# Loading the rows of the projection's first half in two parts

## The chip, the cores and the metric

The kernel runs on one core of a Trainium2 chip. A core has a matrix engine (TensorE, PE in the profile, its weight loads PEld), three engines for element-wise work (VectorE, DVE; ScalarE, ACT; GpSimd, POOL), a sync engine (SyncE, SP) that here only issues transfers, and 16 DMA engines that move data between HBM (DRAM) and the on-chip memory SBUF. Matmul results go to PSUM banks. Each engine takes its own instructions in order and waits for others by semaphores. The metric is the device time of one execution in microseconds.

## The reference

The input `x` is 32 images of 96 channels by 56 by 56, in float32. Two layers run on it, one after the other.

```
layer 0:  h = silu(bn1(conv1x1(x, w1)))            # 96 -> 576 channels
          h = silu(bn2(depthwise3x3(h, w2)))
          s = sigmoid(se2 @ silu(se1 @ mean(h)))    # squeeze and excite, per image
          x1 = x + bn3(conv1x1(h * s, w3))          # 576 -> 96: "the projection"
layer 1:  ca, sa = channel and spatial gates from |rfft2(x1)|, mean and norm of x1
          y  = x1 * ca * sa
          offset, gate, y_base = 3x3 convolutions of y (and of coordinates and |rfft2(y)|)
          y_def = deformable 3x3 convolution of y at the offsets
          z  = (1 - gate) * y_base + gate * y_def
          out = relu(batchnorm over all images (z) + x1)
```

## The kernel before

An image goes through three stages, and the stages of successive images run beside each other. `hidden` (L204) expands and convolves the 576 hidden channels of image b+2. `attend` (L447) projects image b+1 back to 96 channels and works out its gates with Fourier sums. The main loop in `layers` (L953) does the offsets, the sampling and the deformable convolution of image b, in 7 bands of 8 rows. The main loop is cut into slots: after each small piece of the image's own work, `pump` advances the other two stages by a step, so that every engine holds a mixture of the three in an order that is fixed when the program is built. SP's transfers stand in the order in which they are written, too.

**Hidden stage.** The 576 channels are held in nine units (`UNITS`, L75): channels 0 to 511 of the upper half of the image (units 0 to 3), a mixed unit of the last 64 channels with both halves (unit 4), and channels 0 to 511 of the lower half (units 5 to 8). Each unit ends in `acch`, 128 partitions by 28 rows by 56, which ACT finishes (L222) and stores to the DRAM tile `h2d` (L224).

**Projection.** It takes four steps, q = 0 to 3, of seven rows of the upper and seven of the lower half. `project_loads` (L307) brings the rows back: with `half` 0 it loads units 0 to 3 into `hq0` (128 x 4 x 392, 784 KB) and with `half` 1 units 4 to 8 into `hq1` (128 x 5 x 392, 980 KB). Both tiles have one buffer, so the load for q+1 waits until TensorE has read that of q. `project` (L321) multiplies: at L329 four matmuls over `hq0` into one PSUM bank, a step later four over units 5 to 8 of `hq1` into a second bank, then the two of unit 4 (L335). The profile has two records for each such matmul, so that a group of four shows as x8. ACT adds the bias (L339), POOL adds `x` (L476).

In `attend` the order is: matmuls of `hq0`, then the load of the next `hq0`, then the matmuls of `hq1`, then the load of the next `hq1`.

**Sampling weights.** For each band, `offsets` (L654) stores the offsets to DRAM (L668) and loads them back spread over 112 partitions as `ht` (L680, 252 KB). ACT makes hat functions `ho` of it (L686, L688) and stores them as `hd` (L690). `weights_load` (L696) loads them back as `wc` (two loads, L702) and `wr` (L703); VectorE multiplies the two (L709). The sources of `ht` and `wc` are broadcast over a leading dimension of eight. Matmuls at L738 sample with the product, ACT copies the samples into `v` (L742, L749), and L757 is the deformable convolution into the PSUM tile `pd`, of which there is one. VectorE reads `pd` into `z` (L796 to L799), and only then can the matmuls of the next band at L757 write `pd`.

**Transfers.** SP issues the loads of `hq0`, `hq1`, `xt`, `yp`, `ht`, `wc`, `wr` on one queue (q1), ACT the stores of `h2d` and `hd` on another (q10), POOL the rest (q0). SP and ACT share eight completion semaphores in rotation: a transfer waits until the one that stands eight places before it has landed.

Of the kernel before, what the change touches and what calls it, by code (L numbers as in the profile page):

```python
# [33 lines left out]
EW = ER * W  # L34
# [267 lines left out]
def project_rows(p, half):  # L302

    return p["hq"].tile([128, (NCH - 1, len(UNITS) - NCH + 1)[half], EW], FP, name=f"hq{half}")


def project_loads(nc, p, h2d, q, half):  # L307

    u0, u1 = ((0, NCH - 1), (NCH - 1, len(UNITS)))[half]
    hq = project_rows(p, half)  # L310
    nc.sync.dma_start(hq, h2d[u0:u1, :, q * EW : (q + 1) * EW].rearrange("u p n -> p u n"))
    return [(UNITS[u][0], hq[:, u - u0]) for u in range(u0, u1)]


# [132 lines left out]
def attend(tc, p, b, x, h2d, pooled, x1, given=False):  # L447
# [7 lines left out]
    if not given:  # L455
        NQ = HH // ER
        first = project_loads(nc, p, h2d, 0, 0)
        yield from squeeze(nc, p, pooled)
        rows = [first, project_loads(nc, p, h2d, 0, 1)]
        for _ in range(2):  # L460
            yield
        for q in range(NQ):
            at = q, q + NQ
            xrs = [residual_load(nc, p, x, k) for k in at]
            outs = project(nc, p, rows)
            next(outs)
            yield
            if q + 1 < NQ:
                first = project_loads(nc, p, h2d, q + 1, 0)
            yield  # L470
            os = next(outs)
            if q + 1 < NQ:
                rows = [first, project_loads(nc, p, h2d, q + 1, 1)]
            yield
            for k, o, xr in zip(at, os, xrs):
                nc.gpsimd.tensor_tensor(o, o, xr, ALU.add)  # L476
                nc.gpsimd.dma_start(x1[:, k * EW : (k + 1) * EW], o)
            yield
# [1037 lines left out]
```

## Time and profile before

| | |
|---|---|
| three runs | 8979.61, 9001.68, 9002.55 us; median 9001.68 us |
| profiled execution | 8993.57 us, span on the core 8991.8 us |
| mean granted TensorE clock | 0.94 |
| PE busy | 8180.0 us (91% of the span) |
| VectorE busy | 7174.8 us (80%) |
| ScalarE busy | 5380.8 us (60%) |
| GpSimd busy | 2600.4 us (29%) |
| loads of hq0, hq1 | 128 of 784 KB, 128 of 980 KB |
| matmuls at L329 | 2048 records, 796.8 us busy, 99.2 us of idle time before them |

An image takes some 262 us (q = 3 of images 15 and 16 starts at 4157.98 and 4417.24 us). A line of the table of groups or of the timeline gives start, duration, engine, source line, operation and tiles out<-in; a number in square brackets is the idle time of that engine just before, and what is taken to have ended it. A line of the waits gives who waited for whom, microseconds in total, how often, and the longest. Releasers are inferred from semaphore events: a wait for several is put down to the last event that is seen, and that is not always the right one. "Granted clock" is the share of full speed that TensorE is given. Images are counted from 0.

### The profile page before, as it was taken

How to read it: one execution, taken by the hardware profiler on the slowest of the kernel's cores; microseconds unless marked ns; L12 is line 12 of the kernel's file. 1: busy time of each engine (PE TensorE's matmuls, PEld its weight loads, DVE VectorE, ACT ScalarE, POOL GpSimd, SP SyncE). 2: the span in 40 equal slices, each digit the busy share in tenths (PEclk: the TensorE clock that was granted, in tenths of full speed). 3: DMA queues.
4: the chain of work that ended last, by engine and by line, in shares of the span. 5: the costliest groups of instructions: out<-in, count | busy, mean ns of one | idle time of the engine just before them, and what ended most of it. 6: DMA issues, size and time to landing. Idle time of an engine off the chain costs nothing. (4 is left out here: it accounts for less than half of the span.)

```text
span 8991.8 us, 137403 instructions
## 1 busy us (share of the span) xinstructions
PE 8180.0 (91%) x52406; PEld 5185.1 (58%) x52406; DVE 7174.8 (80%) x6821; ACT 5380.8 (60%) x10486; POOL 2600.4 (29%) x2608
## 2 busy tenths in 40 slices
PE   5899999999999999999999999999999999999960
PEld 3456565666656656665666666566566656666640
DVE  7688888888888888888888888888888888887333
ACT  2356666666666666666666666666666666666553
POOL 0133233333323332332332333233333323332210
PEclk9889999999999999999999999999999999999985
DMA  2356666666666666666666666666666666666669
GB/s 80 109 144 167 164 167 164 164 155 155 169 167 167 169 163 150 159 164 167 169 167 160 153 159 166 168 167 168 164 151 162 166 166 168 168 165 146 130 189 417
DMA packets 1068756, 1486.47 MB, mean 165 GB/s; under 512 B 590190, under 2 KB 839838, under 8 KB 1055806
## 3 DMA queue, kind: packets, MB, share of 16 engines
q1 hardware_dynamic: 858995, 985.20, 46.7%
q10 hardware_dynamic: 153803, 329.80, 10.2%
q0 software_dynamic: 55296, 162.60, 6.7%
q8 instruction: 420, 6.88, 0.4%
q14 instruction: 242, 1.98, 0.1%
HBM read 1064.29 MB, written 412.65 MB: 164 GB/s over the span
## 5 line engine op out<-in xcount | busy, mean ns | idle before, releaser
L262 DVE SCALAR_TENSOR_TENSOR acch<-hp,w,acch 128x1512 f32<-128x1512 f32 (+1 forms) x2250 | 4348.3, 1933 | 38.3
L615 PE MATMUL mm<-yp,c_jointW 104*128 104x448 f32 x4032 | 1655.9, 562 | 1.0 <-DMA yp<-fqd 1.0
L720 POOL COPY ybl<-yp 96x448 f32<-96x448 f32 x896 | 1035.1, 1183 | 1541.2 <-PE mm L724 1541.0
L757 PE MATMUL pd<-v,c_def 128*96 128x224 f32 (+1 forms) x6272 | 1429.6, 375 | 53.8 <-DVE z L796 29.0
L757 PEld LDWEIGHTS pd<-v,c_def 128*96 128x96 f32 (+1 forms) x6272 | 1039.5, 173 | 349.1 <-issue 74.5
L615 PEld LDWEIGHTS mm<-yp,c_jointW 104*128 104x128 f32 x4032 | 768.0, 194 | 758.2 <-issue 724.7
L738 PE MATMUL mm<-wc,yt 64*96 64x144 f32 x12544 | 1086.6, 302 | 115.7 <-ACT yb L649 44.8
L738 PEld LDWEIGHTS mm<-wc,yt 64*96 64x96 f32 x12544 | 845.6, 165 | 430.2 <-issue 193.2
L173 ACT ACTIVATE hp<-mm,sh,inv 128x392 f32<-128x392 f32 (+2 forms) x1216 | 812.0, 672 | 461.9 <-PE mm L169 416.4
L169 PE MATMUL mm<-xt,w 96*128 96x392 f32 (+3 forms) x2688 | 1056.8, 527 | 34.4 <-DMA xt<-in_x 33.4
L742 ACT COPY v<-mm 96x288 f32<-96x288 f32 (+1 forms) x2688 | 1003.6, 442 | 126.9 <-PE mm L738 81.4
L329 PE MATMUL mm<-hq,w3s 128*96 128x392 f32 x2048 | 796.8, 536 | 99.2 <-DMA hq<-h2d 92.4
L709 DVE TENSOR_TENSOR wc<-wc,wr 128x1008 f32<-128x1008 f32 x448 | 562.7, 1256 | 365.8 <-DMA wr<-hd 338.6
L644 PE MATMUL mm<-yp,c_base0W 96*64 96x224 f32 x8064 | 827.3, 357 | 0.0
L668 POOL DMA_DIRECT2D od<-at x224 | 185.6, 829 | 2217.9 <-DVE at L664 1515.6
L749 ACT COPY v<-v 32x448 f32<-32x448 f32 x1344 | 755.2, 562 | 29.7
L644 PEld LDWEIGHTS mm<-yp,c_base0W 96*64 96x64 f32 x8064 | 554.0, 135 | 275.4 <-issue 61.5
L726 ACT COPY yt<-mm 128x384 f32<-128x384 f32 (+1 forms) x896 | 350.5, 439 | 544.3 <-PE mm L724 543.8
L635 ACT ACTIVATE hid<-mm,c_dg1b 50x448 f32<-50x448 f32 x224 | 140.6, 628 | 862.9 <-PE mm L615 853.6
L329 PEld LDWEIGHTS mm<-hq,w3s 128*96 128x96 f32 x2048 | 339.1, 174 | 453.1 <-issue 311.0
L222 ACT ACTIVATE acch<-acch,sh,inv 128x1568 f32<-128x1568 f32 x288 | 488.3, 1695 | 180.3 <-DVE acch L262 167.0
L476 POOL TENSOR_TENSOR o<-o,xc 96x392 f32<-96x392 f32 x256 | 374.3, 1462 | 738.9 <-ACT o L339 737.3
(194 smaller groups left out, 9146.8 us busy)
## 6 DMA issues: line engine op xcount, KB each, us to landing
h2d<-acch ACTq DMA_DIRECT2D x288, 784.0 KB
wc<-hd SPq DMA_DIRECT2D x896, 252.0 KB
wr<-hd SPq DMA_DIRECT2D x448, 504.0 KB
hq<-h2d SPq DMA_DIRECT2D x128, 980.0 KB
hq<-h2d SPq DMA_DIRECT2D x128, 784.0 KB
hq<-x1d SPq DMA_DIRECT2D x768, 98.0 KB
ht<-od SPq DMA_DIRECT2D x224, 252.0 KB
hd<-ho ACTq DMA_DIRECT2D x224, 252.0 KB
```

The source lines that it names most:

```text
L169: nc.tensor.matmul(pt[p0 : p0 + w1.shape[1], : rows * W], w1, xts[hf][:, r0 * W : (r0 + rows) * W], start=True, stop=True)
L173: nc.scalar.activation(h1[lo:hi, row0 : row0 + rows, 1 : 1 + W], pt[lo:hi, : rows * W].rearrange("p (h w) -> p h w", h=rows), AF.Silu, bia ...
L262: nc.vector.scalar_tensor_tensor(acc[:, lo:hi], win, wk, acc[:, lo:hi], ALU.mult, ALU.add)
L329: nc.tensor.matmul(pts[half][:C, :EW], w3s[:, ch], hq, start=(i == 0), stop=False)
L615: nc.tensor.matmul(view, weights[:, k], yp[:channels, r0 : r0 + RB, dx + PD - 1 : dx + PD - 1 + W], start=(k == 0), stop=(k == NTAP - 1))
L644: nc.tensor.matmul(pb[i * BC : (i + 1) * BC, : BW // 2].rearrange("p (h w) -> p h w", h=RB // 2), w["base"][:, k], yp[:C, r0 + i * RB // 2 ...
L709: p["tc"].keep_in_program_order(nc.vector.tensor_tensor(wc, wc, wr, ALU.mult))
L720: nc.gpsimd.tensor_copy(yb[:, :, s], blocks)
L738: nc.tensor.matmul(pt[k][:C, (t - lo) * KP : (t - lo + 1) * KP], yt[ps, t], s[ps, t * KP : (t + 1) * KP], start=True, stop=True)
L742: nc.scalar.copy(v[:C, :, lo:hi, k].rearrange("c k t p -> c t k p"), pt[k][:C, : (hi - lo) * KP].rearrange("c (t k p) -> c t k p", t=hi - ...
L749: nc.scalar.copy(v[C:, 1 + 2 * i : 3 + 2 * i], v[i * QC : (i + 1) * QC, KA:])
L757: nc.tensor.matmul(out.rearrange("c q (t x) -> c t q x", x=TS), p["w"]["def"][ks, k], v[ks, k].rearrange("c t s (r x) -> c t (s r) x", r=T ...
```

## The change

The load of `hq0` is issued as two transfers, of units 0 and 1 and of units 2 and 3, one after the other on the same queue. The load of `hq1` remains one.

```
     u0, u1 = ((0, NCH - 1), (NCH - 1, len(UNITS)))[half]
     hq = project_rows(p, half)
-    nc.sync.dma_start(hq, h2d[u0:u1, :, q * EW : (q + 1) * EW].rearrange("u p n -> p u n"))
+    for u, v in ((u0, u1),) if half else ((u0, u0 + 2), (u0 + 2, u1)):
+        nc.sync.dma_start(hq[:, u - u0 : v - u0], h2d[u:v, :, q * EW : (q + 1) * EW].rearrange("u p n -> p u n"))
     return [(UNITS[u][0], hq[:, u - u0]) for u in range(u0, u1)]
```

In the built program the order of the instructions on PE, DVE, ACT and POOL is the same as before. SP has 128 more transfers. The first matmul of each L329 group over `hq0` waits for the first part alone; the third one, the first to read unit 2, has a wait for the second part.

## Prediction

> **What bounds the kernel now.** I read the shares and the clock of the page first, then the waits, then one image in the timeline (image 16, around q = 3).
>
> ```profile
> PE 8180.0 (91%) x52406; PEld 5185.1 (58%) x52406; DVE 7174.8 (80%) x6821; ACT 5380.8 (60%) x10486; POOL 2600.4 (29%) x2608
> ...
> PEclk9889999999999999999999999999999999999985
> ...
> L329 PE MATMUL mm<-hq,w3s 128*96 128x392 f32 x2048 | 796.8, 536 | 99.2 <-DMA hq<-h2d 92.4
> ```
>
> TensorE is nearly always busy at nearly full clock, so time saved on it counts, if nothing else is late next. Its longest wait for a transfer is the one that the change touches: 92.4 us in 30 waits of about 3.1 us.
>
> The timeline of PE, SP, ACT and DVE in image 16 shows where that wait stands, and what runs beside it:
>
> ```profile
> 4386.43 12.84 SPq L311 DMA_DIRECT2D hq<-h2d  x2
> 4401.30 0.66 SPq L680 DMA_DIRECT2D ht<-od  x1
> 4404.94 9.08 SPq L311 DMA_DIRECT2D hq<-h2d  x2
> 4428.75 1.20 SPq L702 DMA_DIRECT2D wc<-hd  x2
> 4430.04 0.54 SPq L703 DMA_DIRECT2D wr<-hd  x1
> ...
> 4409.89 2.87 PE L329 MATMUL mm<-hq,w3s 128*96 128x392 f32 x8
> 4417.24 4.36 PE L329 MATMUL mm<-hq,w3s 128*96 128x392 f32 x8 [2.79 <-DMA hq<-h2d]
> 4447.51 0.94 PE L757 MATMUL pd<-v,c_def 96*96 96x224 f32 x2 [2.30 <-ACT v L749]
> ...
> 4415.30 0.78 ACT L686 ACTIVATE ho<-ht,c_blk 112x576 f32<-112x576 f32 x1 [2.77 <-DMA ht<-od]
> ...
> 4439.56 1.21 DVE L709 TENSOR_TENSOR wc<-wc,wr 128x1008 f32<-128x1008 f32 x1 [3.35 <-DMA wr<-hd]
> 4440.69 5.97 DVE L262 SCALAR_TENSOR_TENSOR acch<-hp,w,acch 128x1568 f32<-128x1568 f32 x3
> 4446.69 0.68 DVE L796 SCALAR_TENSOR_TENSOR z<-pd,c_cvec,yb 96x448 f32<-96x448 f32 x1
> ```
>
> Two things are to be seen. First, the load for q = 3, issued at 4404.94, is 12.3 us under way and TensorE waits for it; a group of eight records that takes 2.87 us elsewhere takes 4.36 us after the pause. Second, 30 us later TensorE waits again, at L757, until VectorE has read `pd` into `z` (the group names ACT, but z ends at 4447.37 and L757 starts at 4447.51). VectorE was late because it waited at 4439.56 for `wr`, and `wr` hangs on a chain of transfers: `ht` issued 4401.30, `ho` at 4415.30, `hd` stored, `wc` and `wr` issued from 4428.75. Nothing in that chain asks for the matmuls of q = 3.
>
> The granted clock around the two pauses (columns: window, its length, busy time of PE, PEld, DVE, ACT, POOL, clock, DMA share, GB/s):
>
> ```profile
> 4416.90:4420.31 3.41, 3.07 (x5) 1.53 (x6) 3.37 (x2) 1.70 (x3) 2.49 (x3) 0.50 1.16 279
> 4420.31:4447.62 27.31, 25.01 (x140) 14.51 (x139) 21.85 (x21) 11.88 (x23) 12.79 (x14) 1.00 0.74 176
> 4447.62:4454.45 6.83, 6.83 (x23) 5.23 (x24) 6.16 (x9) 2.71 (x6) 1.57 (x3) 0.50 1.06 226
> ```
>
> Each pause is paid twice, once as idle time and once as a clock of 0.5 for 3.41 or 6.83 us.
>
> **The change part by part.**
>
> *Issues on SP.* 128 more issues of 0.37 us (median of the 256 at L311) are 47 us of SP's time. Cover: after `hq0` SP stands at the load of `hq1`, which waits for L335 (758.1 us in 96 waits) or for the last `h2d` store. If that cover went, `hq1` would be issued 0.4 us later, and over images 2 to 30 it lands at least 2.6 us before it is read (q = 2; 9 us and more at the others). Cost 0. Bytes and packets are unchanged, and q1 takes them in order.
>
> *Rotation of the semaphores.* With a transfer more, the `wr` issued at 4416.68 would wait for the first part of `hq0` in place of `ht`; the whole `hq0` had landed by 4417.1, so it is at most 0.5 us late, and VectorE multiplies it only at 4432.53. Cost 0.
>
> *The added wait on the third matmul.* Matmuls with a wait already satisfied follow the one before in 329 ns at L246, as those without one do. Cost 0 where the second part has landed.
>
> *q = 0 to 2.* The last packet of `hq0` has passed 16.3 us (q = 0), 8.7 us (q = 1) and 9.5 us (q = 2) before TensorE reads it, in medians over images 2 to 30. No gain.
>
> *q = 3, the earlier start.* TensorE is ready 9.5 us after the issue in each of these images; the wait is 2.43 to 4.11 us, mean 3.15. How much earlier does half the load land? Of the 16 completion marks of this load, one for each DMA engine, eight come about 8 us after the issue and eight only at 11.2 to 12.2 us (image 16). The late eight are held by `ht`, whose packets run until about 9.5 us; their 256 packets of `hq0` pass between about 9.0 and 11.1 us, half of them by about 10.2 us (sums over images 2 to 30). So the first part should land 0.9 us sooner. Bounds: 0 (both parts end with one late engine) and 3.15 us (it lands before TensorE is ready). I take 0.9, since the late engines' packets are the nearest row. The first two matmuls then take 1.3 us (4 of 8 records of 2.87 us, in their spacing of 0.33) or 2.6 us at half clock, longer than 0.9, so the second part is there when the third matmul comes. A shorter pause also has less slow clock: pauses of 2.4 to 2.5 us had 3.41 us of it, the mean over all is 5.06. At 0.44 us lost for each us (image 16: 4.36 - 2.87 = 1.49 us in 3.41) I put this at 0.4. Gain on TensorE 1.3 us an image.
>
> *What is late next.* `z` starts 7.1 us after the product at L709 at the earliest (1.21 and 5.97 us of VectorE). Over images 2 to 30 that limit is met exactly in about half, and `z` comes later than it by 7.9 us in all. So the earlier TensorE can advance L757 by 8 us at most over the run; the rest of 29 x 1.3 = 38 us is waited for at L757. Gain 8 us.
>
> *The clock after L757.* The pause there is 1.31 us now in the mean (0.56 to 3.05) and becomes 1.31 + 1.3 - 0.27 = 2.3 us. Of the nine pauses there of 1.41 to 1.49 us, five brought the slow clock, and all of 2.3 us and over did. Slow time after L757 is now 2.24 us an image; pauses of 2.4 to 2.8 us at q = 3 had 4.7, so for 2.3 I take 4.3. Cost 29 x 0.44 x (4.3 - 2.24) = 26 us. Bounds: 0, and 58 us if each image gets 6.83 us.
>
> *What absorbs it.* 140 us later TensorE waits for VectorE at L724 (19.1 us in 13 waits, 1.5 us each). There a delay of 0.9 us disappears in 13 images: 12 us. Bounds 0 and 26.
>
> Sum: -8 + 26 - 12 = +6 us. On the profiled execution's 8993.57 us this is about 9000 us; the median of the runs is 8.1 us above it, so 9008 us.
>
> **Two rules of the Trainium skill.** The trace has slow clock after pauses of 1.41 to 2.0 us, and its stretches are multiples of 3.41 us. The skill's page "TensorE: Matmul & The Clock Gate" (section on HAM oscillation) gives the same 3.4 us window, but as a rule for authors to have "no PE-idle gaps >~3.4µs". By that rule a pause of 2.3 us would cost no clock, and the sum would be -8 us; the trace decides against it. The page "DMA: Bandwidth & Descriptors" (Rules for kernel authors, and Anatomy of one DMA) speaks against the change: it advises to join transfers, up to 1 MiB each, and counts about 2 us as fixed for each. Estimated from that page, a second part landing 2 us after the whole load does now would be about 0.3 us late at half clock, +9 us in 30 waits; no row here shows such a cost.
>
> **The rivals.**
>
> *The gain reaches the end (faster).* If `z` is not what holds L757, or the chain of `ht`, `hd` and `wr` moves up as well, 1.3 us x 30 = 39 us are saved: 8963 us. For it speaks TensorE's 91%; against it the wait at L757 in nearly every image. A first part landing before TensorE is ready would free 3.15 + 2.0 us, 154 us in all; the late engines exclude most of that.
>
> *The clock after L757 (slower).* Place: L757, 30 us after q = 3. Price: up to 58 us with 6.83 us of slow clock in each image and nothing absorbed, less 8: 9052 us. It decides from 5.0 us of slow time an image: 29 x 0.44 x (5.0 - 2.24) = 35, less 8, is 27 us. For it: every pause of 2.3 us and more has at least one slow window. Against it: the later waits for VectorE.
>
> *Nothing happens.* Both parts land together because the last completion mark comes from one late engine: 0 us, 9002 us.
>
> **How the numbers follow.** A measurement can tell about 0.3%, 27 us, from no change. Chances: my sum 0.28 and "nothing" 0.15, both within it; the slower rival 0.32; the faster 0.25. The 80% range leaves about a tenth out beyond each rival: 8960 to 9046 us; my sum's own range is 8990 to 9027.
>
> **What the changed profile would show.** The wait of L329 for `hq` falls from 3.1 to about 2.2 us, in 30 waits still at q = 3; the third matmul has no wait of its own; the wait at L757 grows by about 1 us and shows slow clock in more than the present 12 images; `wr` lands at the same distance from the load of q = 3. The prediction is wrong if L329's wait vanishes, if the third matmul waits, or if L757 keeps its pause while the image gets shorter.

## The result, and the profile after

The changed kernel takes 9030.81 us (median of six runs, 9021.72 to 9035.16) beside 8994.65 us for the kernel before on the same chip: a ratio of 1.0044, 95% interval 1.0031 to 1.0058, or 36 us more. A second measurement, taken with the experiments below, gave 1.0039 (1.0024 to 1.0054). The change makes the kernel slower by 0.4%.

From L312 on, the changed kernel's lines stand one lower than those of before: L330 is the old L329, L758 the old L757, L797 the old L796. From the page, the shares of the engines and the two groups that changed:

```profile
PE 8191.1 (91%) x52406; PEld 5199.6 (58%) x52406; DVE 7176.8 (80%) x6821; ACT 5384.4 (60%) x10486; POOL 2612.2 (29%) x2608
...
L758 PE MATMUL pd<-v,c_def 128*96 128x224 f32 (+1 forms) x6272 | 1458.7, 380 | 112.2 <-DVE z L797 93.2
...
L330 PE MATMUL mm<-hq,w3s 128*96 128x392 f32 x2048 | 763.2, 517 | 65.1 <-DMA hq<-h2d 33.5
```

The line of the deformable convolution in the page of before:

```profile
L757 PE MATMUL pd<-v,c_def 128*96 128x224 f32 (+1 forms) x6272 | 1429.6, 375 | 53.8 <-DVE z L796 29.0
```

Before, L329 had 796.8 us of work with 99.2 us of idle time ahead of it; now it is 763.2 and 65.1. The projection has become 68 us cheaper. L757 had 1429.6 and 53.8 us; L758 has 1458.7 and 112.2, which is 87 us dearer. That is the case in two lines: the deformable convolution has lost more than the projection has gained.

The waits of TensorE (who for whom: us in all, times, longest) say who does it:

```profile
PE pd L758 <- DVE z L797: 93.2, 30, 5.6
...
PE mm L330 <- DMA hq<-h2d: 33.5, 14, 5.2
PE mm L330 <- ACT ho L687: 30.2, 17, 3.0
```

Two waits of before, for this section and a later one:

```profile
PE pd L757 <- DVE z L796: 29.0, 25, 3.0
...
PE mm L738 <- DVE sq L379: 17.6, 13, 4.9
```

So the wait for `z` was 29.0 us. Of the three lines of after, the second and the third are one wait: both stand at q = 3 and are for the first part of `hq0`. In every image from 2 to 29 the group starts 0.14 us after a completion mark of that part, as it did before after one of the whole load; where an operation of `ho` ends between the two, the profile names `ho`.

Image 16 in the timeline, PE first and then VectorE:

```profile
4439.62 4.54 PE L330 MATMUL mm<-hq,w3s 128*96 128x392 f32 x8 [1.89 <-ACT ho L687]
4452.51 2.88 PE L330 MATMUL mm<-hq,w3s 128*96 128x392 f32 x8
4470.31 0.59 PE L758 MATMUL pd<-v,c_def 96*96 96x224 f32 x2 [2.54 <-DVE z L797]
...
4462.35 1.21 DVE L710 TENSOR_TENSOR wc<-wc,wr 128x1008 f32<-128x1008 f32 x1 [2.64 <-DMA wr<-hd]
4463.48 5.97 DVE L262 SCALAR_TENSOR_TENSOR acch<-hp,w,acch 128x1568 f32<-128x1568 f32 x3
4469.48 0.68 DVE L797 SCALAR_TENSOR_TENSOR z<-pd,c_cvec,yb 96x448 f32<-96x448 f32 x1
```

TensorE now waits 1.89 us at q = 3. The third matmul of the group has no wait of its own: the whole group stands in one line with one idle time. Thirty us later the chain is the old one: VectorE waits for `wr`, then does the product and three long operations, and only then `z`. TensorE is held until `pd` has been read into `z`, in this image for 2.54 us. The clock around the two pauses (window, its length, busy time of PE, PEld, DVE, ACT, POOL, clock, DMA share, GB/s):

```profile
4440.12:4443.53 3.41, 3.41 (x7) 1.46 (x6) 3.38 (x2) 1.96 (x4) 2.25 (x3) 0.50 1.14 299
4443.53:4470.84 27.31, 24.77 (x141) 14.53 (x140) 24.31 (x22) 12.55 (x24) 13.58 (x14) 1.00 0.68 171
4470.84:4477.67 6.83, 6.83 (x24) 4.91 (x22) 5.69 (x9) 1.92 (x5) 1.57 (x3) 0.50 0.98 223
```

I followed TensorE through each image by the number of its instruction and took means over images 2 to 29. Positions count from the moment when TensorE is ready for q = 3, and "lead" is how much earlier than before it reaches the same instruction (minus is earlier):

| | before | after | after, repeat |
|---|---|---|---|
| pause at q = 3, us | 3.18 | 1.98 | 2.20 |
| slow clock within the next 40 records, us | 5.12 | 1.95 | 2.56 |
| lead 40 records after q = 3, us | 0 | -2.45 | -1.96 |
| pause at the deformable convolution, us | 1.30 | 3.34 | 3.03 |
| slow clock from it to record 200, us | 2.19 | 5.97 | 5.12 |
| lead at record 200, us | 0 | +0.90 | +0.84 |
| length of an image against before, us | 0 | +1.17 | +0.94 |

The pause and its slow clock were not removed. They moved 30 us down the image. The lead is used up at `z`, which does not come earlier, and the longer pause there brings more slow clock than it did. Some 29 images of 1.17 us are 34 us; the profiled executions differ by 33 us (spans 9025.0 and 8991.8).

### The profile page after: what moved, and what is told of

The parts are those of the page before. It is cut to its first block, busy times and chain, and to the rows that moved or that the text cites. A ratio compares the mean times of both kernels' runs of the same rounds, so it can differ in the third digit from the quotient of the medians.

```text
span 9025.0 us, 137505 instructions
## 1 busy us (share of the span) xinstructions
PE 8191.1 (91%) x52406; PEld 5199.6 (58%) x52406; DVE 7176.8 (80%) x6821; ACT 5384.4 (60%) x10486; POOL 2612.2 (29%) x2608
## 2 busy tenths in 40 slices
DMA packets 1070806, 1486.49 MB, mean 165 GB/s; under 512 B 592238, under 2 KB 841886, under 8 KB 1057854
## 5 line engine op out<-in xcount | busy, mean ns | idle before, releaser
L758 PE MATMUL pd<-v,c_def 128*96 128x224 f32 (+1 forms) x6272 | 1458.7, 380 | 112.2 <-DVE z L797 93.2
L758 PEld LDWEIGHTS pd<-v,c_def 128*96 128x96 f32 (+1 forms) x6272 | 1056.3, 175 | 417.8 <-issue 118.8
L330 PE MATMUL mm<-hq,w3s 128*96 128x392 f32 x2048 | 763.2, 517 | 65.1 <-DMA hq<-h2d 33.5
L330 PEld LDWEIGHTS mm<-hq,w3s 128*96 128x96 f32 x2048 | 327.3, 168 | 403.0 <-issue 292.0
```

The costliest lines, as they stand in the source:

```text
L330: nc.tensor.matmul(pts[half][:C, :EW], w3s[:, ch], hq, start=(i == 0), stop=False)
L758: nc.tensor.matmul(out.rearrange("c q (t x) -> c t q x", x=TS), p["w"]["def"][ks, k], v[ks, k].rearrange("c t s (r x) -> c t (s r) x", r=T ...
```

## The experiments

Theory A says: only q = 3 matters, and the loss comes from the wait for `z`, which stands on VectorE behind a wait for `wr`.

### The split at q = 3 alone

```
-    for u, v in ((u0, u1),) if half else ((u0, u0 + 2), (u0 + 2, u1)):
+    for u, v in ((u0, u1),) if half or q < 3 else ((u0, u0 + 2), (u0 + 2, u1)):
```

> The load of hq0 is split at q = 3 alone; at q = 0 to 2 it stays one transfer. Theory A (only q = 3 matters: TensorE starts the projection sooner there, and is then stopped longer at the deformable convolution of the next image, with a slow clock after it): the whole slowdown stays, ratio to the kernel before 1.003 to 1.005 (about +36 us), pause before the matmuls of q = 3 2.0 us instead of 3.1, pause at the deformable convolution 3.3 us instead of 1.3. Theory B (the cost is that of 128 more transfers, in SP's issues or in the rotation of semaphores): a quarter of it, ratio about 1.001.

Measured: 1.0024 (1.0012 to 1.0036). The trace has what the theory asks for: 2.05 us of pause at q = 3, 3.06 at the deformable convolution, a lead of -2.00 us that becomes +0.96. The time, though, lies between the two theories: above a quarter of the cost, and somewhat below the whole.

### The split at q = 0, 1 and 2 alone

```
-    for u, v in ((u0, u1),) if half else ((u0, u0 + 2), (u0 + 2, u1)):
+    for u, v in ((u0, u1),) if half or q == 3 else ((u0, u0 + 2), (u0 + 2, u1)):
```

> The load of hq0 is split at q = 0, 1 and 2 alone; at q = 3 it stays one transfer. Theory A: nothing, ratio 0.999 to 1.001, both pauses as in the kernel before (3.1 and 1.3 us). Theory B: three quarters of the slowdown, ratio about 1.003.

Measured: 1.0015 (1.0000 to 1.0029). Both pauses are as before (3.12 and 1.43 us). As the interval begins at 1.000, this was measured again, beside the whole change:

> The split at q = 0, 1 and 2 alone, once more, since 1.0015 with an interval from 1.000 to 1.003 left it open. If the split costs nothing there: ratio 0.999 to 1.001. If it costs about 13 us: 1.001 to 1.002.

> The changed kernel itself, beside the runs of the others on one chip. If the parts add up (q = 3 alone 1.0024, q = 0 to 2 alone 0 to 1.0015): ratio 1.0025 to 1.004. If q = 3 alone and q = 0 to 2 alone do less than both together: 1.0045 and more.

Measured: 1.0017 (1.0000 to 1.0033) and, for the whole change, 1.0039. So the parts add up: 0.24% at q = 3 and about 0.15% at q = 0 to 2, the latter just at the edge of what these runs can tell from nothing. Theory A holds for the larger part of the cost. It does not explain the smaller, which by the medians is 18 us in the first measurement and 5 us in the second.

### z ahead of the product

VectorE's order is set by a planner. This edit makes it place one product of each image, the one that waits for `wr` just before `z` of the last band, behind the first operation of `z`. The order on all other engines stays as it was.

```
 def weights(nc, p, wc, wr):
-    p["tc"].keep_in_program_order(nc.vector.tensor_tensor(wc, wc, wr, ALU.mult))
+    head = p.pop("head", None)
+    with p["tc"].issue_after(head) if head else nullcontext():
+        p["tc"].keep_in_program_order(nc.vector.tensor_tensor(wc, wc, wr, ALU.mult))
...
 def combine(nc, p, j, pd, yb, gate, st):
-    nc.vector.scalar_tensor_tensor(z, pd[:C, :BW], p["w"]["cv"]("def_b"), yb, ALU.add, ALU.subtract)
+    head = nc.vector.scalar_tensor_tensor(z, pd[:C, :BW], p["w"]["cv"]("def_b"), yb, ALU.add, ALU.subtract)
+    if j == NBD - 1:
+        p["head"] = head.ins
```

> The kernel before, with one exchange on VectorE for each image after the first: the first operation of z for the last band (the one that frees pd) now stands ahead of the product at L709 that waits for wr, instead of behind it. The instructions of the other engines are in the same order. Theory A: z no longer waits for wr, the pause of 1.3 us at the deformable convolution and its slow clock (about 1 us) go; if nothing else is late there, up to 29 x 2.3 = 66 us less, ratio 0.993 to 0.998. Theory C (the image's length is set by something later, so that what happens at the deformable convolution is given back): ratio 0.999 to 1.001.

> The same exchange on VectorE, with hq0 loaded in two parts at every q. Theory A: with z no longer behind the wait for wr, what the split gains at q = 3 (1.2 us of pause and 1.2 us of slow clock an image) passes on: 35 to 70 us less than the exchange alone, so faster than the kernel before as well, ratio 0.986 to 0.994. Theory C: the split still costs its 36 us, ratio 1.003 to 1.005.

Measured: 0.9970 (0.9958 to 0.9981) without the split, 0.9951 (0.9935 to 0.9967) with it. With `z` out of the way the sign of the change turns: the split that costs 36 us in the kernel as it was takes 18 us off here (8954.19 to 8936.60 us). That is theory A, though both steps are smaller than it said (theory A allowed up to 66 us for the exchange; it brought 30). The two intervals overlap a little; two more settings below, 0.9977 to 0.9960 in another order of VectorE and 0.9927 with the split at q = 3 alone, have the same sign.

The timeline of the exchange without the split, PE and then VectorE (the quoted lines stand two lower than in the kernel before, from L709 on):

```profile
4416.48 2.81 PE L759 MATMUL pd<-v,c_def 96*96 96x224 f32 x14
4423.49 0.54 PE L759 MATMUL pd<-v,c_def 96*96 96x224 f32 x2
4455.30 0.73 PE L740 MATMUL mm<-wc,yt 64*96 64x144 f32 x8 [2.31 <-DVE sq L379]
...
4414.57 6.80 DVE L262 SCALAR_TENSOR_TENSOR acch<-hp,w,acch 128x1568 f32<-128x1568 f32 x3
4421.58 0.68 DVE L798 SCALAR_TENSOR_TENSOR z<-pd,c_cvec,yb 96x448 f32<-96x448 f32 x1
4422.18 1.19 DVE L711 TENSOR_TENSOR wc<-wc,wr 128x1008 f32<-128x1008 f32 x1
4428.09 0.92 DVE L379 TENSOR_REDUCE sq<-hq 112x56 f32<-112x448 f32 x1 [3.83 <-DMA hq<-x1d]
```

VectorE no longer stands still ahead of `z`, and the deformable convolution at 4423.49 starts without a pause. Over the run:

```profile
PE mm L740 <- DVE sq L379: 50.8, 31, 3.4
...
PE mm L740 <- DVE wc L711: 4.4, 1, 4.4
...
PE pd L759 <- DVE z L798: 0.2, 1, 0.2
```

The wait for `z` fell from 29.0 to 0.2 us, and the wait of the sampling matmuls for the sums at L379 rose from 17.6 to 50.8 us. In means over the images: the pause at the deformable convolution 0.01 us, no slow clock there, a lead of -2.51 us at record 200, of which -0.55 is left at record 360, and an image 0.74 us shorter. So 1.29 us of pause were worth another 1.03 us of clock, and most of both is lost again some 30 us later, where TensorE waits at 4455.30 in the lines above.

### Why most of it is lost again

Two reasons were possible. Either the product is late for someone: in means over the images it starts 30.2 us after the moment when TensorE is ready for q = 3, and 25.3 us after it in the kernel before. Or the sums at L379, which wait for `x1` from DRAM and hold a PSUM bank until they are done, are next in line. This edit puts the product behind two of the three long operations instead, still ahead of `z`, by writing it one slot later in the program:

```
-                        ready.extend(weights(nc, p, *ws) for ws in loads[:1])
-                        del loads[:1]
+                        if n and j == 0 and h:
+                            mine = loads.pop(0)
+                            later.append((slot + 1, lambda mine=mine: ready.append(weights(nc, p, *mine))))
+                        else:
+                            ready.extend(weights(nc, p, *ws) for ws in loads[:1])
+                            del loads[:1]
```

> The kernel before, with another exchange on VectorE for each image after the first: the product at L709 that waits for wr now stands behind two of the three long operations at L262 that used to follow it, and ahead of the third; z follows the third. So VectorE works while wr is under way, z comes as early as in the first exchange, and the product is hardly later than before. In the first exchange TensorE gains 2.4 us at the deformable convolution and gives 1.6 us back 29 us later, at L738. Theory D (it is given back to the chain through x1 in DRAM, whose loads VectorE's sums at L379 wait for, and those hold a PSUM bank): the same gain as the first exchange, ratio 0.996 to 0.998. Theory E (it is given back because the first exchange makes the product 3 us later): nothing is given back, 29 x 2.3 = 66 us less, ratio 0.992 to 0.994.

> The same exchange with hq0 loaded in two parts. Theory D: as the first exchange with the split, ratio 0.994 to 0.996, since the split brings x1 forward by the 1 to 2 us that it gains at q = 3. Theory E: 35 us and more below the exchange alone, ratio 0.987 to 0.990.

Measured: 0.9977 (0.9960 to 0.9993) and 0.9960 (0.9945 to 0.9976). That is theory D; the 0.992 to 0.994 of theory E lies outside the first interval. In the waits of the first of the two, the sums hold TensorE nearly as in the first exchange:

```profile
PE mm L738 <- DVE sq L379: 45.2, 31, 2.3
...
PE mm L738 <- DVE wc L709: 4.7, 1, 4.7
...
PE pd L757 <- DVE z L796: 0.7, 3, 0.3
```

The lead at record 200 is -2.59 us, at record 480 -0.59. The product starts 27.3 us after TensorE is ready for q = 3 here, 2.9 us sooner than in the first exchange and still 2.0 us later than in the kernel before, and TensorE waits for the product itself only once in either run (4.4 and 4.7 us; 4.6 us before). So its lateness explains a small part of the loss at most. That `x1` sets the time of the sums rests on what VectorE was seen to wait for (3.83 us `<-DMA hq<-x1d` above); no run changed that load. With the split, a pause of 1.05 us at the deformable convolution is back in this order, since `z` again stands behind the product: it starts 30.4 us after TensorE is ready for q = 3, beside 29.1 us with `z` first. VectorE hardly waits for `wr` there (0.01 us in the mean); it is its own work ahead of `z` that takes the time.

### The split at q = 3 alone, with z first

If the split at q = 0 to 2 has a price, leaving it out there should show in this setting too. The edit of VectorE's order is the first one; the load is split as in the first experiment, and then in three parts:

```
-    for u, v in ((u0, u1),) if half or q < 3 else ((u0, u0 + 2), (u0 + 2, u1)):
+    for u, v in ((u0, u1),) if half or q < 3 else ((0, 1), (1, 2), (2, u1)):
```

> The first exchange (z ahead of the product) with the load of hq0 split at q = 3 alone. If the split at q = 0 to 2 costs about 14 us, as its two measurements suggest: that much less than the exchange with the split at every q, ratio 0.993 to 0.9945. If it costs nothing: the same, 0.9945 to 0.9965.

> As the one before, with the load of hq0 at q = 3 in three parts, of one, one and two units. If the late eight DMA engines work off the 256 packets of hq0 in order, the first part lands some 0.5 us sooner than with two units, the pause before q = 3 falls from 2.1 to about 1.6 us, and the second matmul waits little: ratio 0.991 to 0.994, up to 15 us less. If a part has a price of its own (an issue, a completion), the second or third matmul waits and nothing is gained: the same or up to 20 us more.

> The first exchange with the split at every q once more, beside the two others on one chip: ratio 0.994 to 0.9965.

Measured: 0.9927 (0.9908 to 0.9946) in two parts at q = 3 alone, 0.9946 (0.9930 to 0.9962) in three, 0.9959 (0.9945 to 0.9973) in two parts at every q. The first is the fastest kernel of this study: 8920.19 us against 8981.73 before, 62 us less. The split at q = 0 to 2 costs here as well, some 24 us by these medians. Image 16 of the fastest kernel, PE (the old L757 is L760 here):

```profile
4371.19 2.84 PE L330 MATMUL mm<-hq,w3s 128*96 128x392 f32 x8 [1.64 <-ACT ho L687]
4382.39 2.87 PE L330 MATMUL mm<-hq,w3s 128*96 128x392 f32 x8
4398.07 0.59 PE L760 MATMUL pd<-v,c_def 96*96 96x224 f32 x2 [0.42 <-DVE z L799]
```

Here a pause of 1.64 us at q = 3 brings no slow clock (2.84 us for the group, as for any other), and 0.42 us are left at the deformable convolution.

Three parts did shorten the pause, from 2.03 to 1.45 us, as forecast, and the lead at record 240 grew from -3.95 to -4.49 us. But the waits of TensorE, first with two parts and then with three, show where it went:

```profile
PE mm L741 <- DVE sq L380: 47.7, 29, 3.7
...
PE mm L741 <- DVE sq L380: 64.3, 30, 4.8
PE mm L330 <- DMA hq<-h2d: 48.8, 33, 4.4
PE pd L760 <- DVE z L799: 13.0, 14, 2.0
```

The wait for the sums is 64.3 us instead of 47.7 with two parts, and at record 480 the lead is -1.21 us instead of -2.25. It is the whole case once more, one wait further on. Whether three parts are slower than two is left open, as the intervals overlap.

**What stays open** is how the split at q = 0 to 2 costs 14 to 24 us. TensorE has no wait for `hq` there, in any of these traces. One difference is the same in each: the last product before q = 3 starts 1.81 to 1.94 us before TensorE is ready in the three profiles where q = 3 alone is split, and 1.09 to 1.31 us before it in the five profiles with the split at every q. VectorE waits longer for `wr` there, 2.6 to 2.8 us instead of 1.9 to 2.1. That this is what costs the time was not shown, and no run separates SP's added issues, the rotation of the semaphores and the added packets (16 for each added transfer) from each other. With the split at q = 0 to 2 alone the product is no later (1.52 and 1.62 us before, against 1.56 in the kernel before).

## Where the prediction was right and where it was wrong, point by point

The measured 9030.81 us lies inside the 80% range of 8960 to 9046 us, and 4 us above the sum's own range of 8990 to 9027. That the wide range holds it says little: it was made to hold a gain of 39 us as well. The prediction took "within 0.3%" for the likeliest, +6 us; measured were +36 and +32. The case that came is the rival "the clock after L757", slower, which was to decide from 5.0 us of slow time an image on: 5.1 to 6.0 us came. By the steps:

- *Issues on SP, rotation of the semaphores, q = 0 to 2: cost 0.* Probably wrong, by about 14 us, as two measurements of that part alone say (1.0015 and 1.0017, both with an interval that begins at 1.000). The packets are not unchanged either: 1070806 beside 1068756, of which 2048 are on q1, 16 for each of the 128 added transfers. No wait of TensorE for `hq` appeared at q = 0 to 2, as predicted; the cost, if it is one, is elsewhere.
- *The added wait on the third matmul: 0.* Right. No wait there.
- *q = 3, the earlier start.* Right in kind, too small in size. The idle part is 1.0 to 1.2 us (forecast 0.9). The clock part was put at 0.4 us, and it is 0.9 to 1.25: slow clock at q = 3 fell from 5.12 to between 1.95 and 2.80 us an image. The lead is 2.0 to 2.45 us instead of 1.3.
- *What is late next: z, 8 us at most.* Right. The advance of the deformable convolution was 0.40 us an image in the changed kernel and 0.23 in its repeat, 7 to 12 us in all. Exchanging `z` and the product, and nothing else, turned the sign of the split.
- *The clock after L757: 26 us.* The mechanism was right and the term too small, for two reasons that belong together: the pause became 3.0 to 3.3 us, not 2.3, as the lead was larger, and the slow clock after it 5.1 to 6.0 us, not 4.3. From the lead that goes in, the pause that comes and the lead left at record 200, the clock there costs 1.1 to 1.3 us an image: 31 to 38 us.
- *What absorbs it: -12 us at L724.* This step failed, and it made the sign of the sum doubtful. The wait at that place was 19.1 us in the run before, 23.7 us in the first profile after, and 15.9 and 16.3 us in the repeat and in the split at q = 3 alone. From record 200 to the end of the image the delay went from +0.90 to +1.17, from +0.84 to +0.94, and from +0.96 to +0.83 us. In between, at record 480, it was 0.51, 0.49 and 0.56 us: nearly all that was absorbed was lost again. With 0 there, the sum is what is left at record 200, 24 to 28 us in 29 images; about 14 for q = 0 to 2 make it 38 to 42 us, a little above the measured 32 and 36.
- *The gain reaches the end (faster).* It did not come; the 30 waits for `z` in the profile after show why. It did come once `z` was moved.
- *What the changed profile would show.* The pause at q = 3 fell to 1.98 us (forecast 2.2), the third matmul did not wait, and slow clock after the deformable convolution came in 23 of 28 images, where before it were 11. The pause there grew by 2.0 us in place of 1. `wr` stayed where it was, as forecast: the product that waits for it starts 24.9 us after TensorE is ready for q = 3, before it was 25.3.
- *The rule of the Trainium skill* ("TensorE: Matmul & The Clock Gate", section on HAM oscillation) to have no gaps above some 3.4 us, read as leaving shorter ones without a cost, would have given -8 us. These runs do not agree with that reading. Over all thirteen profiles, images 2 to 29, pauses at the deformable convolution of 0.15 to 1 us brought slow clock before record 200 in 1 of 79 images (that one was of 1.00 us), those of 1.4 to 1.7 us in 24 of 33, and those of 2.3 to 3.4 us in 30 of 32.
- *The rule that joins transfers* ("DMA: Bandwidth & Descriptors", Rules for kernel authors) was weighed as +9 us through the second part landing late. In the two profiles of the changed kernel the second part was never late (with `z` first once, by 0.19 us); the page's 2 us are fitted to transfers that GpSimd issues, and these are issued by SP. Yet the split at q = 0 to 2, where TensorE gains nothing by it, seems to cost some 14 us, so the advice points the right way here, by another way than the one worked out.

## What to carry to other kernels

Before a wait is shortened, look for the next place at which the same engine waits for another one whose time does not depend on it: if there is one nearby, the gain only moves there. A moved pause was not neutral here, because where it had grown to 2 us and more it came with its own slow clock. Move what holds the next wait first, and shorten the first wait after that: the same split then gains instead of losing, and it gains most where it is made only in the one place that waits.

## What the runs showed that I had not expected

- A pause of TensorE costs nearly twice its length in these images: with 1.29 us of pause removed at the deformable convolution, 2.19 us of slow clock went too, and with it another 1.03 us. It is not proportional for a single pause there: below 1 us slow clock came once in 79 images, from 2 us on in 79 of 81.
- One exchange of two instructions on VectorE, an engine that is 80% busy, is worth 0.30% of the whole kernel; with the split at q = 3 alone it is 0.73%.
- Splitting transfers whose consumer does not wait was probably not free: 0.15% to 0.3% for 96 more transfers, in three comparisons, two of them with an interval that begins at no change.
